# Where the score scale, the output bias, the zeros and the output tiles of a two-layer transformer are placed, with a new order table

## The chip, the cores and the metric

The kernel runs on one core of a Trainium2 chip. The metric is the device time of one execution in microseconds (us). Times of single parts come from one execution taken by the hardware profiler. Engines: TensorE (PE, and PEld for its weight loads), VectorE (DVE), ScalarE (ACT), GpSimd (POOL) and SyncE (SP, which here only issues transfers). L12 is line 12 of the kernel file of before.

## The reference

Two layers on x of 2 x 1024 x 256, everything in float32. The first is single-head causal attention with a residual, then a layer norm. The second is a block with 16 heads and a dense mixture of four experts, with residuals, then a layer norm again.

```python
x = layernorm(x + attn(x))            # one head, key size 256, gamma/beta on its input
h = x
z = layernorm(h) * ln1_w + ln1_b
q, k, v = z @ wq + bq, z @ wk + bk, z @ wv + bv     # 16 heads of 128
q, k = rope(q), rope(k)
p = softmax(causal(q @ k.T / sqrt(128)))
h = h + (p @ v) @ wo + bo
z = layernorm(h) * ln2_w + ln2_b
top2 = softmax of the two largest of softmax(z @ w_gate)
h = h + sum over 4 experts of top2[e] * (gelu(z @ we1[e] + be1[e]) @ we2[e] + be2[e])
out = layernorm(h)
```

## The kernel before

**Rows.** A row is one tile of 128 queries. The first layer has 16 (class RowA, 2 batches x 8), the second 256 (class RowB, 32 units of batch and head with 8 rows each, numbered 16 to 271). Two units of one group of weights and one batch make a pair of 16 rows. A row goes through `scores` (TensorE, L1206), a mask and the row's maximum (DVE, `softmax_row`, L678 and L680), `exponential` (ACT, L685), `normalise` (DVE's reciprocal L1221, ACT L1223), `transpose` (DVE, L721, 32x32 blocks into a place) and, for every four rows, `gather` (16 transfers issued by SP, L732, in two halves, which finish the transposition into pT) and `output` (TensorE, L1272; the result leaves PSUM through ACT with the value bias, L1288). The exponentials of three rows can be alive (`PR = 3` buffers named pr), the scores of two.

**Projections.** The second layer's wk, wq and wv are multiplied in 2x2 blocks with seven products instead of eight (`seven_products`, p1 to p7, L973 and L982, added up by DVE at L1015), and wo likewise (`seven_outputs`, L1130, added into h by DVE at L1139). The sums of weight blocks that they need are made on POOL (`weight_sums`, L949 to L952; `output_weight_sums`, L1099 to L1102), those of x by `x_sums`, those of the attention's output by `output_sums` (DVE). Only the first pair uses plain projections (`b_project`, `b_value`). After q or k is there, POOL rotates it for rope in pieces of 512 columns (`rotation`, four instructions, L897 to L899); the rows' scores read the rotated tiles Twq and Twk.

**What the change touches.** `scale_queries` multiplies the loaded block of wq by 1/sqrt(128) on POOL (L886); `parameters` copies the transposed parameter vectors from PSUM to the tile par (L588) and scales bq in it (L593). `h_load` brings one batch of the first layer's output from DRAM into h (SP, L856) and `h_bias` adds bo to one tile of h on POOL (L861, 16 times). The places into which the first layer's rows are transposed are set to zero by two memsets on POOL (L710). `a_norm` normalises x for the first layer (L560, DVE). `o_stats`, `m_rstd` and `o_finish` are the last layer norm of each tile: statistics on DVE (L551, L552), the reciprocal root on ACT (L556, L557), a factor on DVE (L1796), the application on ACT (L1801) and the output transfer issued by ACT (L1806). `expert` multiplies by we2 (L1769) and adds into h on DVE (L1778). `load_experts` (SP, L1567, 1 MB) and `load_second` (POOL's queue) bring the experts' weights.

**Order.** Engines run their instructions in the order in which they are issued. Every step above is appended to a list by `do` in a natural order (`at`, `late` and the like put it beside a row). Then a table moves single steps, each ahead of another one:

```python
def ordered(ops, moves):
    names = [key for key, _ in ops]
    for key, before in moves:
        names.remove(key)
        names.insert(names.index(before), key)
    by_name = dict(ops)
    return [by_name[key] for key in names]
```

Names read as in "RowB.gather 39 1" (row 39, second half), "wk.1.0 p4" (group 1, batch 0, product 4), "rotation 12" (the 13th piece rotated), "o_finish 1 1 3" (batch 1, second half, last tile).

Of the kernel before, what the change touches and what calls it, by code (L numbers as in the profile page):

```python
# [28 lines left out]
    ("o_finish 1 1 1", "o_stats 1 1 2"),  # L29
    ("m_rstd 1 4", "m_rstd 1 5"),  # L30
    ("all_of 1 1 1", "expert 1 1 2.0.3.0"),
    ("m_rstd 1 0.1.2.3 #2", "hidden 1 1 3"),
    ("o_stats 1 0 0.1.2.3", "hidden 1 1 1"),
    ("hidden 1 0 3", "m_bias 1 2.3"),
    ("o_stats 0 1 0.1.2.3", "m_bias 1 0.1"),
    ("hidden 1 0 2", "o_stats 0 1 0.1.2.3"),
    ("hidden 0 1 2", "all_of 0 1 1"),
    ("o_stats 0 0 0.1.2.3", "all_of 0 1 0"),
    ("m_rstd 1 4.5.6.7", "o_stats 0 0 0.1.2.3"),
    ("m_residual 1 0.1.2.3", "m_residual 0 0.1.2.3"),  # L40
    ("x1_back 1", "m_residual 1 0.1.2.3"),
    ("m_residual 0 4.5.6.7", "x1_back 1"),
    ("b_output 7 1 4.5", "hidden 0 1 1"),
    ("m_bias 0 6.7", "all_of 0 0 3"),
    ("RowB.output 271 99", "gate_products 1 2.3"),
    ("x1_back 0", "m_rstd 1 0.1.2.3"),
    ("RowB.transpose 271", "m_stats 1 0.1.2.3"),
    ("b_output 7 1 2.3", "RowB.normalise 271"),
    ("RowB.exponential 271", "RowB.output 263 9"),
    ("RowB.normalise 270", "RowB.transpose 269"),  # L50
    ("RowB.normalise 269", "RowB.transpose 268"),
    ("m_bias 0 0", "RowB.exponential 270"),
    ("RowB.output 263 8", "m_bias 0 0"),
    ("RowB.exponential 269", "hidden 0 0 1"),
    ("gate_weights 0", "load_weights 7 wo #2"),
    ("RowB.exponential 268", "gate_weights 0"),
    ("RowB.transpose 266", "gate_best 0 1"),
    ("RowB.normalise 267", "RowB.transpose 266"),
    ("RowB.output 259 8", "RowB.normalise 267"),
    ("RowB.gather 263 1", "RowB.normalise 266"),  # L60
    ("load_second 3", "RowB.gather 263 1"),
    ("RowB.transpose 265", "load_second 3"),
    ("b_output 6 1 6", "gate_products 0 6.7"),
    ("b_output 6 1 2", "RowB.gather 263 0"),
    ("gate_products 0 2.3", "b_output 6 1 0"),
    ("RowB.output 255 9", "gate_products 0 2.3"),
    ("RowB.transpose 263", "RowB.scores 265"),
    ("RowB.transpose 262", "m_transposed 0 1 1"),
    ("hidden 0 0 0", "RowB.transpose 262"),
    ("b_output 6 1 1", "RowB.output 255 8"),  # L70
    ("RowB.normalise 262", "b_output 6 1 1"),
    ("RowB.transpose 261", "RowB.scores 263"),
    ("gate_products 0 0.1", "RowB.normalise 261"),
    ("RowB.gather 259 1", "RowB.exponential 262"),
    ("RowB.transpose 260", "RowB.gather 259 1"),
    ("b_output 6 1 3", "RowB.scores 262"),
    ("RowB.transpose 259", "RowB.exponential 261"),
    ("m_transposed 0 0 0", "RowB.normalise 259"),
    ("m_transposed 0 0 1", "RowB.exponential 260"),
    ("wv.7.1 p5", "RowB.output 251 8"),  # L80
    ("RowB.gather 255 1", "m_norm 0 1"),
    ("m_stats 0 4.5.6.7", "RowB.normalise 257"),
    ("RowB.gather 255 0", "RowB.normalise 256"),
    ("wv.7.1 p4", "RowB.gather 255 0"),
    ("wv.7.1 p3", "wv.7.1 p4"),
    ("wv.7.1 p2", "RowB.output 247 10"),
    ("RowB.scores 257", "RowB.normalise 255"),
    ("RowB.exponential 256", "RowB.transpose 254"),
    ("m_norm 0 0", "RowB.exponential 256"),
    ("m_rstd 0 0.1.2.3", "m_norm 0 0"),  # L90
    ("RowB.scores 256", "m_stats 0 0.1.2.3"),
    ("RowB.output 247 8", "load_weights 6 wo #2"),
    ("RowB.transpose 252", "RowB.exponential 255"),
    ("RowB.gather 251 0", "RowB.gather 251 1"),
    ("RowB.exponential 254", "wo.7.0 12+c"),
    ("RowB.normalise 253", "RowB.transpose 251"),
    ("RowB.exponential 252", "RowB.normalise 253"),
    ("output_sums 7 0 3", "wo.7.0 12+a"),
    ("wo.7.0 22c", "wo.7.0 11b"),
    ("RowB.normalise 251", "wo.7.0 11a"),  # L100
    ("wq.7.1 p7", "rotation 125"),
    ("output_sums 7 0 2", "RowB.scores 251"),
    ("weight_sums wv #10", "output_sums 7 0 2"),
    ("RowB.scores 252", "RowB.gather 247 1"),
    ("wq.7.1 p6", "rotation 124"),
    ("RowB.scores 250", "RowB.gather 247 0"),
    ("RowB.exponential 249", "RowB.normalise 248"),
    ("RowB.transpose 247", "output_sums 7 0 0"),
    ("wq.7.1 p4", "RowB.transpose 247"),
    ("wq.7.1 p2", "load_weights 7 wv #2"),  # L110
    ("RowB.output 239 9", "wq.7.1 p2"),
    ("RowB.output 239 8", "rotation 122"),
    ("wq.7.1 p1", "RowB.output 239 8"),
    ("RowB.scores 248", "RowB.transpose 245"),
    ("rotation 121", "RowB.gather 243 1"),
    ("RowB.normalise 245", "RowB.transpose 244"),
    ("RowB.scores 247", "RowB.normalise 245"),
    ("RowB.scores 246", "RowB.normalise 244"),
    ("wv.0.1 p4", "wv.0.1 p3"),
    ("load_weights 2 wq", "rotation 29"),  # L120
    ("weight_sums wv #2", "load_weights 2 wq"),
    ("h_bias 1 4", "wv.1.1 p7"),
    ("RowB.output 39 10", "RowB.gather 47 0"),
    ("RowB.transpose 47", "wv.1.1 p3"),
    ("RowB.scores 50", "RowB.transpose 47"),
    ("RowB.transpose 46", "RowB.scores 50"),
    ("RowB.exponential 49", "wv.1.1 p4"),
    ("RowB.gather 43 1", "RowB.exponential 48"),
    ("wv.1.1 p2", "RowB.gather 43 1"),
    ("RowB.exponential 47", "wv.1.1 p1"),  # L130
    ("load_weights 1 wo", "RowB.scores 48"),
    ("RowB.output 39 9", "wo.0.0 21+a"),
    ("load_weights 0 wq", "RowB.output 39 9"),
    ("RowB.normalise 46", "load_weights 0 wq"),
    ("rotation 23", "RowB.normalise 46"),
    ("h_bias 1 6", "rotation 23"),
    ("RowB.exponential 46", "h_bias 1 6"),
    ("RowB.output 39 8", "wo.0.0 22+a"),
    ("h_bias 1 2", "RowB.output 39 8"),
    ("wo.0.0 12+c", "RowB.scores 46"),  # L140
    ("RowB.scores 47", "wo.0.0 12+c"),
    ("output_sums 0 0 3", "RowB.scores 47"),
    ("wo.0.0 12+a", "output_sums 0 0 3"),
    ("RowB.normalise 45", "RowB.normalise 44"),
    ("RowB.gather 43 0", "RowB.normalise 45"),
    ("h_bias 1 1", "RowB.scores 45"),
    ("RowB.normalise 43", "RowB.exponential 44"),
    ("RowB.exponential 43", "wo.0.0 11a"),
    ("h_bias 1 7", "wq.1.1 p7"),
    ("RowB.scores 44", "h_bias 1 7"),  # L150
    ("RowB.transpose 42", "RowB.scores 44"),
    ("h_bias 1 3", "RowB.transpose 42"),
    ("RowB.transpose 41", "h_bias 1 3"),
    ("h_bias 1 5", "RowB.transpose 41"),
    ("RowB.normalise 41", "h_bias 1 5"),
    ("RowB.normalise 42", "RowB.normalise 41"),
    ("RowB.exponential 42", "RowB.output 35 8"),
    ("rotation 21", "RowB.exponential 42"),
    ("h_bias 1 0", "rotation 20"),
    ("RowB.transpose 40", "h_bias 1 0"),  # L160
    ("output_sums 0 0 1", "RowB.gather 39 0"),
    ("wq.1.1 p2", "wq.1.1 p4"),
    ("RowB.exponential 41", "wq.1.1 p2"),
    ("RowB.normalise 39", "RowB.transpose 38"),
    ("RowB.normalise 40", "RowB.normalise 39"),
    ("RowB.output 31 10", "RowB.normalise 40"),
    ("output_sums 0 0 0", "RowB.output 31 10"),
    ("RowB.exponential 39", "wq.1.1 p1"),
    ("rotation 19", "RowB.exponential 39"),
    ("load_weights 0 wk", "rotation 19"),  # L170
    ("RowB.transpose 37", "load_weights 0 wk"),
    ("RowB.scores 40", "rotation 18"),
    ("RowB.scores 39", "RowB.scores 40"),
    ("RowB.output 31 8", "RowB.scores 39"),
    ("h_load 1", "wk.1.1 p7"),
    ("h_bias 0 7", "RowB.normalise 37"),
    ("rotation 17", "h_bias 0 7"),
    ("RowB.gather 35 1", "RowB.transpose 36"),
    ("h_bias 0 4", "RowB.transpose 35"),
    ("RowB.scores 38", "h_bias 0 4"),  # L180
    ("h_bias 0 5", "RowB.scores 38"),
    ("RowB.normalise 35", "h_bias 0 5"),
    ("RowB.normalise 36", "RowB.transpose 34"),
    ("wk.1.1 p5", "RowB.normalise 36"),
    ("wk.1.1 p6", "wk.1.1 p5"),
    ("h_bias 0 6", "wk.1.1 p6"),
    ("wk.1.1 p3", "h_bias 0 6"),
    ("wk.1.1 p4", "wk.1.1 p3"),
    ("h_bias 0 3", "wk.1.1 p1"),
    ("RowB.gather 31 1", "h_bias 0 3"),  # L190
# [183 lines left out]
def kernel(  # L374
# [334 lines left out]
    for z in blocks_a:  # L709
        nc.gpsimd.memset(z, 0.0)  # L710
# [1258 lines left out]
```

## Time and profile before

| | before |
|---|---|
| median of 4 runs | 1163.16 us (1157.45 to 1167.78) |
| the profiled execution, its own time | 1161.47 us |
| its span in the profile | 1159.6 us |
| mean granted TensorE clock | 0.994 |
| TensorE busy | 1131.6 us (98%) |
| DVE, ACT, POOL busy | 851.1, 645.1, 812.4 us (73%, 56%, 70%) |
| first layer | about 0 to 165 us |
| pairs of the second layer, each | 55.76 us, to about 1065 |
| last matmul to the end of the span | 7.0 us |

In the profile, "busy" counts the time in which an engine's instructions run. Slices are fortieths of the span with a digit for the busy share in tenths; PEclk is the clock granted to TensorE, in tenths of full speed. In a table by stretches each row names a stretch in us from the span's start, its length, the busy time and number of instructions of each engine, the granted clock, the share of the DMA engines and the GB/s that they moved. A line of waits reads: engine, operation and line that waited, what released it, and then the total us, how often, and the longest. A line of a timeline reads: start, duration, engine, line, operation, output and inputs.

### The profile page before, as it was taken

The numbers are of one execution on the slowest core, as the hardware profiler recorded it, in microseconds if no ns is written. First come the engines' busy times: TensorE is split into PE (matmuls) and PEld (weight loads), VectorE is DVE, ScalarE is ACT, GpSimd is POOL, SyncE is SP. The second block draws the span as 40 slices with busy tenths as digits, with TensorE's granted clock in tenths as the row PEclk, the third lists the DMA queues.
The fourth block names the chain that finished last, engine by engine and source line by source line (L and its number), as shares of the span: only waits on it lengthen the run. The fifth ranks groups of instructions, "written<-read, shape, count | busy, mean of one in ns | idle before, by whom it ended". The sixth has DMA issues, their size and how long they took to land.

```text
span 1159.6 us, 15853 instructions
## 1 busy us (share of the span) xinstructions
PE 1131.6 (98%) x4628; PEld 719.3 (62%) x4628; DVE 851.1 (73%) x1806; ACT 645.1 (56%) x1227; POOL 812.4 (70%) x762
## 2 busy tenths in 40 slices
PE   8999989999999999999999999999999999899997
PEld 5676645566666656565757575757565656566765
DVE  5657786868686868686878777787868687585575
ACT  3434566565656565656565666565665565462444
POOL 6006999999997989698969878888989997002100
PEclk9999999999999999999999999999999999899999
DMA  6142364756545554555455555555555748423011
GB/s 187 37 109 51 112 172 101 166 128 135 118 116 126 119 137 116 118 128 118 114 124 136 125 115 128 133 138 121 140 130 128 159 113 186 98 54 110 1 37 37
DMA packets 243223, 133.91 MB, mean 115 GB/s; under 512 B 18909, under 2 KB 241185, under 8 KB 242369
## 3 DMA queue, kind: packets, MB, share of 16 engines
q1 hardware_dynamic: 237952, 122.89, 45.6%
q0 software_dynamic: 1776, 4.89, 1.5%
q10 hardware_dynamic: 3408, 5.11, 1.2%
q8 instruction: 38, 0.62, 0.2%
q14 instruction: 49, 0.39, 0.1%
HBM read 22.71 MB, written 4.19 MB: 23 GB/s over the span
## 4 chain that ended last, share of the span: by engine, by line
PE 87%; POOL 5%; DVE 3%; DMA 1%; SPq 1%; ACT 1%; issue 1%; ACTq 0%; DVEq 0%; POOLq 0%
PE av L1272 20%; PE sc L1206 19%; PE pa L982 10%; PE pa L973 6%; PE pa L1130 5%; PE pa L1746 5%; PE pe L1769 4%; PE pc L982 4%; PE sc L751 3%; PE pc L973 2%; POOL rot L897 2%; PE pc L1130 2%; PE pa L800 1%; SPq L732 1%; PE pa L660 1%; PE pa L1082 1%
## 5 line engine op out<-in xcount | busy, mean ns | idle before, releaser
L1223 ACT ACTIVATE pr<-pr,rs 128x128 f32<-128x128 f32 (+5 forms) x252 | 195.7, 780 | 225.9 <-DVE rs L1221 225.9
L1206 PE MATMUL sc<-Twk,Twq 128*128 128x512 f32 (+3 forms) x768 | 289.4, 487 | 4.3 <-ACT pr L685 2.7
L1272 PE MATMUL av<-pT,vg 128*128 128x512 f32 (+3 forms) x768 | 270.8, 490 | 6.1 <-DMA pT<-pair_sb 6.1
L685 ACT ACTIVATE pr<-sc,nmx 128x256 f32<-128x256 f32 (+7 forms) x272 | 200.8, 738 | 120.3 <-DVE nmx L680 90.9
L1272 PEld LDWEIGHTS av<-pT,vg 128*128 128x128 f32 x768 | 143.6, 191 | 130.6 <-issue 95.8
L897 POOL TENSOR_TENSOR rot<-Twk,rope_sb 64x512 f32<-64x512 f32 x128 | 167.5, 1309 | 72.6 <-DVE Twk L1015 55.7
L1206 PEld LDWEIGHTS sc<-Twk,Twq 128*128 128x128 f32 x768 | 135.9, 191 | 124.6 <-issue 107.1
L680 DVE TENSOR_REDUCE nmx<-sc 128x1 f32<-128x128 f32 (+7 forms) x272 | 206.1, 758 | 9.4
L897 POOL TENSOR_TENSOR rot<-Twq,rope_sb 64x512 f32<-64x512 f32 x128 | 167.0, 1305 | 10.4 <-ACT Twq L925 1.7
L678 DVE TENSOR_TENSOR sc<-sc,limit 128x128 f32<-128x128 f32 x272 | 79.3, 292 | 97.4 <-PE sc L1206 77.3
L721 DVE STREAM_TRANSPOSE x<-pr 128x640 f32<-128x640 f32 (+1 forms) x124 | 128.5, 1036 | 21.5 <-ACT pr L1223 15.9
L898 POOL TENSOR_TENSOR Twk<-Twk,rope_sb 128x512 f32<-128x512 f32 x64 | 86.0, 1344 | 5.0
L899 POOL TENSOR_TENSOR Twk<-Twk,rot 128x512 f32<-128x512 f32 x64 | 85.6, 1337 | 5.0
L898 POOL TENSOR_TENSOR Twq<-Twq,rope_sb 128x512 f32<-128x512 f32 x64 | 82.1, 1283 | 5.0
L899 POOL TENSOR_TENSOR Twq<-Twq,rot 128x512 f32<-128x512 f32 x64 | 81.7, 1276 | 5.0
L1638 POOL TENSOR_TENSOR hx<-hx,x 128x256 f32<-128x256 f32 x16 | 11.5, 755 | 92.2 <-DMA x<-x_dram 74.6
L721 DVE STREAM_TRANSPOSE pair_sb<-pr 128x128 f32<-128x128 f32 (+1 forms) x120 | 59.9, 500 | 3.3 <-ACT pr L1223 1.9
L1139 DVE TENSOR_TENSOR hx<-hx,pa 128x512 f32<-128x512 f32 x70 | 46.6, 679 | 17.9 <-PE pa L1130 17.9
L1746 PE MATMUL pa<-xT,we_flat 128*128 128x512 f32 x128 | 58.2, 601 | 0.0
L1769 PE MATMUL pe<-lent,hT 128*128 128x256 f32 x240 | 54.4, 380 | 0.0
L1288 ACT ACTIVATE aT_sb<-av,par 128x512 f32<-128x512 f32 x64 | 43.7, 683 | 18.8 <-PE av L1272 14.6
L685 ACT ACTIVATION_READ_ACCUMULATOR pr<-sc,nmx 128x1 f32 x272 | 53.6, 197 | 0.0
(216 smaller groups left out, 1829.4 us busy)
## 6 DMA issues: line engine op xcount, KB each, us to landing
pT<-x SPq DMA_DIRECT2D x496, 128.0 KB, 2.7
pT<-pair_sb SPq DMA_DIRECT2D x480, 64.0 KB, 2.0
pT<-aT_sb SPq DMA_DIRECT2D x48, 128.0 KB, 3.1
pT<-za SPq DMA_DIRECT2D x48, 64.0 KB, 2.1
wq_g<-in_L_ffn_wq_dram SPq DMA_DIRECT2D x9, 256.0 KB, 3.1
wk_g<-in_L_ffn_wk_dram SPq DMA_DIRECT2D x9, 256.0 KB, 3.0
wv_g<-in_L_ffn_wv_dram SPq DMA_DIRECT2D x9, 256.0 KB, 3.0
wo_g<-in_L_ffn_wo_dram SPq DMA_DIRECT2D x9, 256.0 KB, 3.0
```

The costliest lines, as they stand in the source:

```text
L680: nc.vector.tensor_reduce(nmx, sc[:, :L], AX.X, ALU.max, negate=True)
L685: nc.scalar.activation(pr[:, :L], sc[:, :L], AF.Exp, bias=nmx, accum_out=sm)
L721: nc.vector.transpose(z[:, i % 4, :n, :], pr[:, : n * 32].rearrange("p (m s) -> p m s", s=32))
L897: nc.gpsimd.tensor_tensor(rot[lo, :], t[hi, cs], rope_sb[hi, 1, cs], ALU.mult)
L898: eng.tensor_tensor(t[:, cs], t[:, cs], rope_sb[:, 0, cs], ALU.mult)
L899: nc.gpsimd.tensor_tensor(t[:, cs], t[:, cs], rot, ALU.add)
L982: nc.tensor.matmul(pa, lhsT=w, rhs=x, start=start, stop=True, skip_group_check=True)
L1206: nc.tensor.matmul(sc[:, ds(n0, n)], lhsT=qT[:, ts(i, P)], rhs=kT[:, ds(n0, n)], start=True, stop=True,)
L1223: nc.scalar.activation(self.pr[:, :L], self.pr[:, :L], AF.Copy, scale=rs)
L1272: nc.tensor.matmul(cut(av), lhsT=vg[g, b][:, c, ts(hh, HD)], rhs=cut(pT[:, c, :]), start=(c == 0), stop=(c == i),)
L1746: nc.tensor.matmul(ph, lhsT=we1_sb[:, e, c, ts(m, P)], rhs=x2T[:, c, ds(k0 * P, 512)], start=(c == 0), stop=(c == DC - 1),)
L1769: nc.tensor.matmul(pe[:, ts(n, D)], lhsT=hTs[b, j, e][:, c, ts(k, P)], rhs=we2_sb[e][:, c, :], start=(c == 0), stop=(c == IC - 1),)
```

## The change

- **Scale.** `scale_queries` is gone. 128 to the power -1/4 (`ROOT_B`) is multiplied into ln1_w, ln1_b, bq and bk in the parameter tile, so the second layer's normalised input carries the factor and q and k each bear it once. v bears it too, and the attention's output takes it out again when it leaves PSUM.
- **bo.** `h_bias` is placed beside other rows: its 16 steps were moved by the old table to rows 26 to 48, and now stand beside rows 50–53, 66–69, 82–85 and 98–101, after the first addition into the tile.
- **Zeros.** Only the parts of the places that a gather reads and no transpose writes are set to zero, by six smaller memsets on DVE.
- **Output tiles.** Each half batch has its own output tile, whose parts are filled and sent. The very last tile is normalised by `ln_apply` on DVE and sent by SP.
- **Natural order.** a_norm 0 0 stands ahead of parameters 0. The experts 2 and 3 of the last tiles are separate steps, and m_rstd comes after o_finish of the tile before.
- **Order table.** MOVES is another list: the old one has 323 lines and the new one 261 in the diff, some of them shown.

```diff
@@ MOVES, from the end of the program to its start
-    ("o_finish 1 1 1", "o_stats 1 1 2"),
-    ("m_rstd 1 4", "m_rstd 1 5"),
-    ("all_of 1 1 1", "expert 1 1 2.0.3.0"),
+    ("o_finish 1 1 0", "expert 1 1 3.2"),
+    ("o_stats 1 1 1", "m_rstd 1 4"),
+    ("expert 1 1 3.1", "expert 1 1 3.0"),
...
-    ("RowB.gather 255 1", "m_norm 0 1"),
-    ("RowB.gather 255 0", "RowB.normalise 256"),
-    ("wv.7.1 p4", "RowB.gather 255 0"),
+    ("m_stats 0 0.1.2.3", "load_experts"),
...
+    ("RowB.exponential 174", "wq.5.0 p5"),
+    ("RowB.scores 174", "RowB.exponential 174"),
+    ("RowB.exponential 127", "wq.3.1 p5"),
+    ("RowB.scores 127", "RowB.exponential 127"),
+    ("RowB.exponential 91", "wq.2.1 p6"),
+    ("RowB.scores 91", "RowB.exponential 91"),
...
-    ("h_bias 1 6", "rotation 23"),
-    ("h_load 1", "wk.1.1 p7"),
-    ("RowB.gather 35 1", "RowB.transpose 36"),
+    ("RowB.gather 35 1", "output_sums 0 0 0"),
...
-    ("weight_sums wv", "rotation 10"),
-    ("output_weight_sums", "load_weights 1 wv"),
-    ("scale_queries #2", "a_residual 1 1"),
+    ("rotation 12", "RowB.normalise 26"),
+    ("a_apply 1 1 2.3", "RowB.scores 23"),
+    ("weight_sums wk", "a_residual 1 1"),
...
@@ scale
-    SCALE_B = 1.0 / math.sqrt(HD)
+    ROOT_B = HD**-0.25
@@ parameters
-            c = cols["bq"]
-            bq_par = par[:, c : c + wq.shape[1] // P]
-            nc.vector.tensor_scalar(bq_par, bq_par, SCALE_B, None, ALU.mult)
+            for lo, hi in (("ln1_w", "ln2_w"), ("bq", "bv")):
+                t = par[:, cols[lo] : cols[hi]]
+                nc.vector.tensor_scalar(t, t, ROOT_B, None, ALU.mult)
@@ zeros
-    for z in blocks_a:
-        nc.gpsimd.memset(z, 0.0)
+    for j, z in enumerate(blocks_a):
+        z = z.rearrange("p (c b x) -> p c b x", b=4, x=P)
+        for c in range(1, 4):
+            nc.vector.memset(z[:, 4 * j + c, :, : 32 * c], 0.0)
@@ scale_queries
-    def scale_queries():
-        t = wg["wq"].rearrange("p c n -> p (c n)")
-        nc.gpsimd.tensor_scalar(t, t, SCALE_B, None, ALU.mult)
@@ RowB.output
-            nc.scalar.activation(dst, src, AF.Identity, bias=par[:, bcol : bcol + 1])
+            nc.scalar.activation(
+                dst, src, AF.Identity, bias=par[:, bcol : bcol + 1], scale=1.0 / ROOT_B
+            )
@@ natural order of the start
+    do(a_norm, 0, 0)
     do(parameters, 0)
-    do(a_norm, 0, 0)
@@ h_bias
-            late(A0 + HL[b] + 3 + i, h_bias, b, i)
+            n = b * NT + i
+            late(A0 + HB + 2 * NT * (n // 4) + n % 4, h_bias, b, i)
@@ o_finish
-        o = xn_tile()
+        if (b, j) not in outs:
+            outs[b, j] = xn_tile()
+        o = outs[b, j][:, ks[0] : ks[0] + n, :]
...
+        last = (b, tiles[-1]) == (B - 1, NT - 1)
+        if last:
+            i = tiles[0]
+            ln_apply(
+                o[:, 0, :], h[:, b * NT + i, :], mv_h[b][:, i, 0:1], rstd_h[b][:, i : i + 1]
+            )
...
-        nc.scalar.dma_start(dst, o[:, :n, :])
+        (nc.sync if last else nc.scalar).dma_start(dst, o)
@@ natural order of the end
-        do(expert, 1, 1, [(2, k), (3, k)])
+        do(expert, 1, 1, [(2, k)])
+        do(expert, 1, 1, [(3, k)])
         do(o_stats, 1, 1, [k])
-        do(m_rstd, 1, [4 + k])
         if k:
             do(o_finish, 1, 1, [k - 1])
+        do(m_rstd, 1, [4 + k])
```

## The prediction

> **What bounds the kernel now.** I read the page's totals first, then its slices, the table by stretches, the waits of TensorE in the stretches where it sits idle, and the queues that it waits for there.
>
> ```profile
> span 1159.6 us, 15853 instructions
> PE 1131.6 (98%) x4628; PEld 719.3 (62%) x4628; DVE 851.1 (73%) x1806; ACT 645.1 (56%) x1227; POOL 812.4 (70%) x762
> POOL 6006999999997989698969878888989997002100
> PEclk9999999999999999999999999999999999899999
> PE 87%; POOL 5%; DVE 3%; DMA 1%; SPq 1%; ACT 1%; issue 1%; ACTq 0%; DVEq 0%; POOLq 0%
> ```
>
> TensorE is busy 98% of the span and carries 87% of the chain that ended last. POOL looks relaxed at 70%, but it is full from slice 4 on, and the chain runs through it for 5%. I priced each matmul by its usual distance to the next start in the trace (0.4295 us for 512 columns, 0.3225 for 384, 0.2155 for 256, 0.1115 for 128): 1115.7 us. The first starts at 3.5, 33.3 us lie lost between them, and 7.0 us follow the last: 1159.5. The changed order issues the same 4628 matmuls, so the 1115.7 stays. The question is which of the other 44 us go.
>
> ```profile
> core 0: us, PE busy (x) PEld busy (x) DVE busy (x) ACT busy (x) POOL busy (x), PEclk, DMA share, GB/s
> 120.00:140.00 20.00, 19.46 (x82) 14.65 (x80) 14.76 (x30) 10.89 (x23) 18.88 (x16) 1.00 0.32 103
> 140.00:180.00 40.00, 33.09 (x112) 17.47 (x113) 32.22 (x63) 25.55 (x48) 37.69 (x41) 1.00 0.62 153
> 220.00:250.00 30.00, 27.91 (x145) 20.14 (x144) 20.20 (x41) 15.82 (x30) 28.59 (x29) 0.94 0.62 132
> 350.00:930.00 580.00, 580.00 (x2455) 362.89 (x2454) 442.50 (x872) 349.29 (x668) 492.85 (x452) 1.00 0.55 128
> 980.00:1000.00 20.00, 16.02 (x50) 8.48 (x48) 8.77 (x19) 9.94 (x14) 0.44 (x1) 0.83 0.54 118
> ```
>
> Half of the program (350 to 930) loses nothing that shows here; by the distances it loses 0.24 us in each pair of units (55.76 us). The losses are 6.6 us before 20, 2.1 in 120–140, 7.3 in 140–180, 4.0 in 220–250, 1.5 in 930–960 and 6.9 in 980–1000. The waits of TensorE in three of these stretches:
>
> ```profile
> PE sc L1206 <- ACT pr L685: 2.0, 2, 1.4
> PE pc L982 <- POOL S L949: 1.9, 1, 1.9
> PE pt L566 <- DVE pair_sb L560: 1.8, 2, 1.0
> PE sc L1206 <- POOL Twq L899: 1.5, 1, 1.5
> ```
>
> **The opening, 105 to 177.** POOL has no gap here from rotation 2 (105.65) to the end of rotation 12 (177.05). Its queue holds six rotations, the scaling of wq, the sums of wk and wq, two rotations, the sums of wo and wv, three rotations:
>
> ```profile
> 139.30 1.49 POOL L886 TENSOR_SCALAR wq_g<-wq_g 128x512 f32<-128x512 f32 x1
> 140.88 0.46 POOL L949 TENSOR_TENSOR S<-wk_g 128x128 f32<-128x128 f32 x1
> 155.45 0.91 POOL L1099 TENSOR_TENSOR we_flat<-wo_g 128x128 f32<-128x128 f32 x1
> 175.79 1.26 POOL L899 TENSOR_TENSOR Twq<-Twq,rot 128x512 f32<-128x512 f32 x1
> ```
>
> The product p4 of wk waits for 140.88, behind the scaling, and the scores of row 32 for the last line. The change takes scale_queries out of this queue (1.57 with its gap) and puts the sums of wo and wv, 5.2 us (155.45 to 160.71), behind rotation 12; rotation 2 starts some 0.9 later, since TensorE reaches its projection 0.86 us of matmuls later. So rotation 12 ends near 177.05 + 0.9 − 1.6 − 5.2 = 171.1. The same matmuls that lie ahead of the scores of 32 take until 154.7 by distances alone. With POOL as the limit the offset is 171.1 − 154.7 ≈ 16.3, against 19.84 now: **−3.55** in all for 120–180. The waits for DVE's L560 and ACT's L685 shrink for nothing: POOL is late next. The output bias h_bias (16 x 0.73 = 11.3 us of POOL in 177–251) leaves this stretch too.
>
> What pays for it: h_bias comes back as four instructions (2.9 us) in each of the four pairs in about 270–430. POOL's fullest pair (263.00 to 318.76) is 52.56 busy of 55.76; less 1.49 for a scaling and plus 2.9 it is 54.0, so it fits, with 1.8 left. DVE's residual add (L1139) must wait for the h_bias of its tile, and DVE's softmax work stands behind it; the bias stands about 12 us ahead of the next add of the same batch, more than POOL's lag. Cover gone, it would cost up to 2.9 per pair. Value 0.
>
> **Scale.** The scaling runs 11 times, 16.4 us, but after 250 POOL is not waited for, so there it is worth nothing. In its place stand one DVE instruction on some columns of the parameters (L593's row is 0.17) and a scale operand in L1288's ACTIVATE (0.683, the same instruction): 0.
>
> **The start.** The zeros were two memsets on POOL, 1.82 and 3.53 us at 13.21 to 18.48; now six small ones stand on DVE, idle until 5.15. Not shown in the trace; between 6 x 0.17 and the whole 5.35 they end about when the first data come: 0 to +0.5, taken 0. a_norm 0 0 ahead of parameters 0 saves two DVE steps of 0.21, and a_norm 0 1 no longer runs 1630 ns beside the memset (405 usually): **−0.5**.
>
> **Gathers.** Two TensorE waits are for a gather of 16 transfers on SP, one at 226.4 and one at 984.9:
>
> ```profile
> PE av L1272 <- DMA pT<-pair_sb: 2.1, 1, 2.1
> PE av L1272 <- DMA pT<-pair_sb: 4.0, 1, 4.0
> ```
>
> The same stretches by clock (the figure before the DMA share) just after these waits:
>
> ```profile
> 230.00:233.50 3.50, 3.50 (x12) 2.39 (x11) 0.66 (x2) 0.29 (x2) 3.34 (x4) 0.51 0.11 25
> 988.00:994.50 6.50, 5.45 (x7) 2.35 (x8) 3.74 (x8) 3.43 (x5) 0.00 (x0) 0.50 0.39 93
> ```
>
> At 226.4 the attention output of rows 36–39 waits 2.25 us and the granted clock then falls to 0.5 for 3.4 us, 1.6 us more, plus 0.4 close by. Gather 35 starts at 199.9 and pushes gather 39 to 211.9–224.6. In the new order h_load 1 sits between the halves of gather 35, gather 35 starts near 192 and gather 39 has landed by 221, while TensorE comes to it after 223: **−4.1**. If only half of the lead is real the wait shrinks below 1: −3.
>
> *A rule against a row.* The Trainium skill, "TensorE: Matmul & The Clock Gate", section "HAM oscillation — how this bites in real kernels", has the clock fall back only after idle gaps of more than about 3.4 us. Here it fell after 2.25 us. By the rule closing the gap returns 2.25 and no clock, some 1.6 less; I keep the row.
>
> At 984.9 gather 255 (12.75 us of issue from 968.84, against 10.5 for others) shares the transfers with the 1 MB of expert weights issued just ahead of it; 4.15 idle and 2.7 of half clock follow. The new order leaves the load ahead of the gather, while TensorE arrives with 1.34 us less work before it and the gather some 0.4 earlier: **+0.9**. At 947 and 957 two short waits (0.69, 0.50) are broken up by other work put between: **−1.2**.
>
> **The tail.** The last matmul ends at 1152.66. The last tile's expert 3 is split off from expert 2, so one of two adds (0.5) moves under matmuls; the last tile goes through DVE, without L1796 (0.16), without the 0.47 that ACT's L1801 stood behind its predecessor and an issue, and its transfer goes out by SP, whose last gather is issued by about 1050. The landing stays (about 3 us): **−1.4**, between −1.0 and −1.9. Own places for output tiles free a wait that the trace does not show: 0.
>
> **The rest of the table.** From 350 to 930 rows and products are shuffled in some 15 pairs. At most 0.24 x 13 = 3 us can be won. Some rows (127, 174, 91) are scored up to four rows early and hold one of three pr buffers meanwhile; the row's chain through DVE and ACT takes 2.6 to 3.0 us, a row's period is 3.49, so it just fits. Bounds −3 and +4.3 (one stall like that at 226); taken **+2**, nearer the stall, since the row's margin is only half a microsecond.
>
> **Sum:** −3.55 − 0.5 − 4.1 + 0.9 − 1.2 − 1.4 + 2 = −7.9. The profiled execution took 1161.5 (span 1159.6 and 1.9 around it): 1153.6. The median of the four runs is 1163.2, 1.7 above; I put the median of the changed kernel about half of that higher, **1154.5**. Its own range is 1150 to 1159. One per cent is 11.6 us, about what a measurement of this kernel tells from no change: bounds 1151.5 and 1174.8.
>
> **Rivals.** *The wait at 985 goes too* (15%). For it: gather 255 needs only 4 us; against it: the load stays in front. −6.9 − 0.9 more: 1147. *POOL was not the limit of the opening* (15%): rows through DVE and ACT (32.22 of 40 busy) end last, −3.55 and −0.5 fall away: 1158.5. Against it: the chain names POOL's rotations from 160.7 to 177.1 without a break. *The filled pairs give it back* (16%): POOL at 54.0 of 55.76 lags in four pairs by 2 us each: 1162.5. *Slower* (12%): a row scored early takes the buffer, the row behind it exponentiates late, its gather starts late, and TensorE waits with a half-clock stretch after. One such stall costs 4.3 (2.25 + 1.6 + 0.4). From five of the 15 pairs on it decides: 5 x 4.3 = 21.5, 1176. Against it: DVE and ACT are 76% and 60% busy in 350–930, so a late row is caught up.
>
> **How the numbers follow.** The forecast has 42%. Below 1151.5 lie the first rival and a third of the forecast's own range: 30%. Above 1174.8 lies nearly all of the slow case: 12%. The rest, 58%, is within 1%. The range 1144 to 1168 leaves out the slow case and the lower end of the first rival.
>
> **What would show it.** Right: no L886 row; POOL's rotation 12 ends near 171 and TensorE's lost time before 180 falls from 16 to 12; no wait for a gather at 220–230 and one clock dip fewer; about 4 to 5 us idle still at 980–990; under 6 us after the last matmul. Wrong: TensorE waits on POOL in 270–430, or on gathers between 350 and 930, or no wait at 985.

## The result, and the profile after

The changed kernel takes 1161.39 us (median of 46 runs, 1158.54 to 1167.50) against 1163.17 (70 runs, 1157.20 to 1170.62): ratio 0.9981, interval 0.9968 to 0.9993. It is faster by 1.8 us, or 0.2%. Forecast were 8.7. The profiled execution took 1161.38, its span is 1159.5, 0.1 below that of before.

The page's totals, POOL's and the clock's slices and the chain that ended last, changed kernel:

```profile
span 1159.5 us, 15802 instructions
PE 1128.5 (97%) x4628; PEld 716.6 (62%) x4628; DVE 853.7 (74%) x1813; ACT 648.9 (56%) x1228; POOL 790.6 (68%) x749
POOL 4006999989897979697969778887989998002100
PEclk9999999999999999999999999999999999999999
PE 86%; DVE 8%; DMA 2%; issue 1%; POOL 1%; ACT 1%; SPq 1%; DVEq 0%; ACTq 0%; POOLq 0%
```

POOL fell from 5% of the chain to 1%, and DVE rose from 3% to 8%. What TensorE waits for is now mostly VectorE instead of POOL. The clock has no slice below 9 any more. The same stretches as before (start and length, then busy time and instructions by engine, granted clock, DMA share, GB/s):

```profile
20.00:120.00 100.00, 98.75 (x367) 64.77 (x366) 68.99 (x167) 38.46 (x91) 22.23 (x19) 1.00 0.28 66
140.00:180.00 40.00, 34.37 (x116) 18.00 (x115) 34.66 (x67) 28.80 (x56) 37.77 (x37) 1.00 0.60 151
220.00:250.00 30.00, 30.00 (x156) 21.03 (x155) 21.66 (x47) 17.41 (x34) 26.87 (x31) 1.00 0.68 137
350.00:930.00 580.00, 576.81 (x2435) 360.24 (x2434) 439.93 (x868) 349.09 (x665) 482.66 (x447) 1.00 0.55 126
980.00:1000.00 20.00, 16.44 (x64) 9.43 (x63) 11.03 (x24) 11.86 (x18) 2.29 (x3) 1.00 0.51 121
```

Before, the first of them read:

```profile
20.00:120.00 100.00, 100.00 (x379) 66.43 (x378) 69.60 (x172) 41.55 (x96) 27.75 (x23) 1.00 0.31 74
```

220–250 is full now, the dip at 980–1000 is smaller. But 20–120 and 350–930, which had been full, have holes: 1.25 and 3.2 us of TensorE. In the lost time of the prediction (matmul starts against their usual distances), us:

| stretch | before | after | difference | forecast |
|---|---|---|---|---|
| 0–20 | 6.6 | 6.1 | −0.5 | −0.5 |
| 20–120 | 0.4 | 3.2 | +2.8 | 0 |
| 120–180 | 9.4 | 7.4 | −2.0 | −3.55 |
| 180–250 | 4.7 | 1.1 | −3.7 | −4.1 |
| 250–920 | 3.8 | 8.8 | +5.0 | +2 |
| 920–960 | 1.5 | 2.9 | +1.5 | −1.2 |
| 960–1000 | 6.9 | 3.9 | −3.0 | +0.9 |
| last matmul to the end | 7.0 | 6.6 | −0.4 | −1.4 |

The profile of before holds three stretches of 3.41 us at half clock ahead of the last matmul (one at 230, two at 988), that of the changed kernel none. As the last section shows, such a stretch depends on where a wait falls in the execution, too.

TensorE's waits (what released it, total, times, longest), the main ones in 140–165, in 350–930 and in 900–1000:

```profile
PE sc L1143 <- ACT pr L624: 4.3, 4, 1.9
...
PE pa L919 <- DVE Twq L952: 3.2, 4, 1.5
...
PE av L1209 <- DMA pT<-pair_sb: 1.9, 1, 1.9
PE av L1209 <- issue: 1.9, 1, 1.9
PE pa L1685 <- DVE hx L1029: 1.7, 1, 1.7
```

Neither POOL's sums nor its rotations stand here any more. The scores wait for a buffer that an exponential frees, whose row waited for its mask on VectorE. The second line is product p7 of wq: TensorE waits for VectorE to empty a bank. The next two are the attention's outputs behind gathers 239 and 255; the second of them is put down to no engine. VectorE's queue ahead of such a wait, at 381 to 387 (start, duration, engine, line, operation, tiles):

```profile
382.81 1.75 DVE L1049 TENSOR_TENSOR aT_sb<-aT_sb 128x512 f32<-128x512 f32 x1
384.49 0.29 DVE L617 TENSOR_TENSOR sc<-sc,limit 128x128 f32<-128x128 f32 x1
384.81 0.69 DVE L619 TENSOR_REDUCE nmx<-sc 128x1 f32<-128x512 f32 x1
385.41 0.68 DVE L952 TENSOR_TENSOR Twq<-pc,part 128x512 f32<-128x512 f32 x1
```

The mask and the maximum of row 91, whose scores the new table puts ahead of p6, stand in front of the addition into Twq. In the trace of before that addition directly follows the 1.75 us one:

```profile
384.63 1.75 DVE L1112 TENSOR_TENSOR aT_sb<-aT_sb 128x512 f32<-128x512 f32 x1
386.31 0.68 DVE L1015 TENSOR_TENSOR Twq<-pc,part 128x512 f32<-128x512 f32 x1
```

### The profile page after: what moved, and what is told of

It reads as the page before. It is cut to its first block, busy times and chain, and to the rows that moved or that the text cites. A ratio compares the mean times of both kernels' runs of the same rounds, so it can differ in the third digit from the quotient of the medians.

```text
span 1159.5 us, 15802 instructions
## 1 busy us (share of the span) xinstructions
PE 1128.5 (97%) x4628; PEld 716.6 (62%) x4628; DVE 853.7 (74%) x1813; ACT 648.9 (56%) x1228; POOL 790.6 (68%) x749
## 4 chain that ended last, share of the span: by engine, by line
PE 86%; DVE 8%; DMA 2%; issue 1%; POOL 1%; ACT 1%; SPq 1%; DVEq 0%; ACTq 0%; POOLq 0%
PE sc L1143 19%; PE av L1209 18%; PE pa L919 10%; PE pa L910 5%; PE pa L1067 5%; PE pa L1685 5%; PE pe L1708 4%; PE pc L919 4%; PE pa L741 2%; PE sc L692 2%; PE pc L910 2%; PE pc L1067 2%; PE pa L599 1%; PE pa L586 1%; PE pa L1019 1%
## 5 line engine op out<-in xcount | busy, mean ns | idle before, releaser
L1160 ACT ACTIVATE pr<-pr,rs 128x128 f32<-128x128 f32 (+3 forms) x252 | 195.6, 778 | 187.8 <-DVE rs L1158 187.7
L624 ACT ACTIVATE pr<-sc,nmx 128x640 f32<-128x640 f32 (+7 forms) x272 | 201.2, 740 | 153.6 <-DVE nmx L619 120.0
L619 DVE TENSOR_REDUCE nmx<-sc 128x1 f32<-128x640 f32 (+7 forms) x272 | 206.1, 758 | 9.4
L1076 DVE TENSOR_TENSOR hx<-hx,pa 128x512 f32<-128x512 f32 x70 | 46.6, 679 | 13.8 <-PE pa L1067 13.7
L1225 ACT ACTIVATE aT_sb<-av,par 128x512 f32<-128x512 f32 x64 | 43.8, 685 | 20.5 <-PE av L1209 18.9
```

Source lines behind the costliest of these rows:

```text
L619: nc.vector.tensor_reduce(nmx, sc[:, :L], AX.X, ALU.max, negate=True)
L624: nc.scalar.activation(pr[:, :L], sc[:, :L], AF.Exp, bias=nmx, accum_out=sm)
L1160: nc.scalar.activation(self.pr[:, :L], self.pr[:, :L], AF.Copy, scale=rs)
```

## The experiments

Lost time of each run's profile, us. "Code, old order" and the like are the runs below; those for which no median is given were run once. Stretches that an edit doesn't reach agree mostly within 0.3, except where a half-clock stretch follows a wait in one run and not in another (about 1.6 us each). Two stretches scatter more: 250–920 loses 3.8 in before and 2.7 to 3.1 in four other runs with the old order and the early bias (only before waits 0.92 at 331), and 960–1000 loses 2.5 to 3.9 in the changed kernel and the runs with its order that have no half clock there.

| run | 0–20 | 20–120 | 120–180 | 180–250 | 250–920 | 920–960 | 960–1000 | span |
|---|---|---|---|---|---|---|---|---|
| before | 6.6 | 0.4 | 9.4 | 4.7 | 3.8 | 1.5 | 6.9 | 1159.6 |
| before + scale | 6.3 | 0.5 | 7.7 | 4.7 | 2.7 | 1.5 | 7.2 | 1156.6 |
| before + scale + late sums | 12.3 | 1.4 | 6.6 | 4.7 | 3.1 | 0.9 | 6.0 | 1161.1 |
| before + late bias | 6.4 | 0.4 | 9.5 | 3.1 | 4.5 | 1.5 | 4.1 | 1155.9 |
| before + zeros | 6.3 | 0.4 | 13.7 | 2.8 | 2.7 | 1.5 | 6.6 | 1159.8 |
| code, old order | 6.4 | 0.4 | 7.7 | 2.9 | 2.8 | 1.5 | 5.4 | 1152.1 |
| after | 6.1 | 3.2 | 7.4 | 1.1 | 8.8 | 2.9 | 3.9 | 1159.5 |
| after + scaling work | 6.1 | 3.2 | 8.2 | 1.6 | 8.2 | 2.7 | 3.1 | 1159.1 |
| after, early bias | 6.4 | 3.2 | 7.4 | 0.6 | 8.1 | 2.7 | 6.2 | 1160.7 |
| after, old opening | 6.2 | 0.4 | 8.3 | 1.3 | 8.6 | 4.0 | 3.6 | 1158.6 |
| after, x sums later | 6.8 | 3.2 | 6.0 | 0.0 | 7.8 | 4.1 | 3.9 | 1157.8 |
| after, natural middle | 6.1 | 3.2 | 7.4 | 1.0 | 4.4 | 1.5 | 4.7 | 1154.4 |
| after, gather 239 | 5.9 | 3.2 | 9.0 | 1.3 | 8.6 | 0.2 | 2.5 | 1156.5 |
| after, load split | 6.3 | 3.2 | 7.4 | 1.0 | 8.6 | 4.3 | 2.6 | 1159.3 |
| after, root first | 6.7 | 3.2 | 7.5 | 1.0 | 8.9 | 2.8 | 3.3 | 1158.7 |
| mixed order, split | 6.2 | 0.4 | 6.8 | 1.3 | 4.5 | 1.5 | −0.2 | 1145.4 |

**Is it the code or its order?** The changed code with the steps in the order of the kernel before:

```diff
 MOVES = (
-    (the new table)
+    (a table that gives the old order; the experts 2 and 3 of a tile stand next to each other)
 )
```

> The changed code in the old order: scale, zeros, output tiles and the DVE finish of the last tile as changed, all steps in the order of the kernel before (the bias early too, the experts 2 and 3 of a tile next to each other). Theory V (the table brought the new waits): lost time 350-930 is back at 2.2 us from 6.6, 20-120 at 0.4 from 3.2, while the waits at 226 (2.3 and the half clock) and 985 are as before; the tail after the last matmul is below 6 us, since the last reciprocal root stands ahead of the application of the tile before. Span about 1157, 2 to 3 below before. Rival (the moved work itself, not its order, makes the new waits): 350-930 stays at 5 or more.

Median 1153.87 of 7 runs, ratio 0.9903 (0.9868 to 0.9938): 6.5 us of lost time less than in the changed kernel and 0.9 less behind the last matmul. 350–930 is full again:

```profile
350.00:930.00 580.00, 580.00 (x2439) 361.33 (x2438) 442.12 (x871) 350.37 (x668) 482.08 (x443) 1.00 0.55 128
```

Theory V's points on 20–120, on 350–930 and on the tail came true. The waits at 226 and 985 stayed too, but 2.11 and 3.75 long and with less half clock behind them (none and 3.41 us), and the span was 5 lower than it said. The same code is worth 1%, and the new table gives most of it back.

**The middle of the table.** 79 of its lines, those beside rows 57 to 231, are taken out; three of them are shown.

```diff
-    ("wv.6.1 p3", "RowB.output 231 10"),
...
-    ("RowB.scores 91", "RowB.exponential 91"),
...
-    ("wq.0.1 p5", "output_sums 1 0 3"),
```

> The changed kernel without the 79 lines of the new table that move steps beside rows 57 to 231, which stand in their natural order again; the late bias stays. Theory V (rows whose scores were put ahead of products bring their mask and maximum into VectorE's queue ahead of the additions that free TensorE's banks): the waits of product p7 of wq at 273, 328, 385, 443, 778 and 836 (6.2 us together) fall to 0.15 each, but for 0.3 and 0.9 at the first two, as before; 250-930 loses 3.5 instead of 8. Theory H (the bias on POOL in rows 50 to 101 slows VectorE beside it): the four waits between 270 and 445 (4.5 us) stay, those at 778 and 836 go.

Median 1157.17 of 12 runs, ratio 0.9930 (0.9904 to 0.9956); 250–920 loses 4.4 instead of 8.8. The p7 waits at 328 and 385 fell from 1.56 and 1.63 to 0.43 each, that at 778 from 1.35 to below 0.2. Waits of TensorE in 250–400:

```profile
PE pa L840 <- DVE Twq L873: 1.1, 3, 0.6
```

So these lines cost 4.4 us; that the rows put forward among them do it is read from VectorE's queue above, not tested row by row. What is left over the old order's 2.7 to 3.1, with p7 waits of 0.74 and then 0.43 in the four pairs with the late bias instead of about 0.13, is the bias's share.

**The bias, both ways.** In the kernel before its sixteen steps were put where the changed kernel has them, and in the changed kernel back where they were.

```diff
+    ("h_bias 0 0", "RowB.scores 51"),     # before: late
...
+    ("h_bias 0 1", "RowB.transpose 26"),  # after: early
```

> The kernel before with nothing changed but the place of the sixteen bias additions: beside rows 50 to 101, as in the changed kernel. Two things are asked. Where the wait at 226 went (2.25 us and the half clock): if the bias on POOL made it, lost time 220-250 falls from 4.0 to below 1; if the order of h_load 1 and gather 35 made it, it stays at 4. And what the bias costs in its new place: by the prediction on record nothing (POOL has 1.8 us of slack in a pair); by theory H (POOL beside VectorE in the pairs) each p7 of wq in the four pairs after 270 waits 0.3 us or more longer, lost time 250-500 from 2.1 to above 3.3.

> The changed kernel with the sixteen bias additions back beside rows 26 to 48, all else as changed. Theory H: the p7 waits between 270 and 445 (0.86, 1.56, 1.63, 0.42) lose 0.3 each, 250-500 falls from 5.0 to about 3.8, and POOL, 11.3 us fuller in 177-250, makes rows wait there: 180-250 rises from 1.05 to 2 or more. Rival (the bias is hidden in both places): every stretch within 0.3 of the changed kernel.

In the kernel before, the late bias alone brings the wait at 226 down from 2.25 to 0.5 without half clock, for a new wait of 1.1 at 212.7: 180–250 falls from 4.7 to 3.1. In the changed kernel the early bias does not bring the wait back (0.6). So it takes both, the full POOL and the old order; the prediction named only the order (of gather 35 and h_load 1, which no run moves alone), and either change removes it. The late bias has a price where nothing was forecast: in the kernel before the p7 waits of the four pairs are 0.78, 0.41, 0.43 and 0.42, against 0.13 or so in the runs with the early bias. That makes 1.8 us in 250–920 against the 2.7 of two other runs of the old order, 0.7 against the profile of before with its wait at 331. In the changed kernel the early bias wins back 0.7. Whether POOL beside VectorE is the reason, as theory H says, is not shown.

**The scale, both ways.**

```diff
-        nc.gpsimd.tensor_scalar(t, t, SCALE_B, None, ALU.mult)   # before: gone
+        nc.gpsimd.tensor_scalar(t, t, 1.0, None, ALU.mult)       # after: back
```

> The kernel before with the scale moved and nothing else: the eleven POOL instructions of scale_queries are gone, the order of all other steps is the old one. Prediction on record: POOL is without a gap from 105 to 177, so its queue ends 1.57 us earlier and the lost time in 120-180 falls from 9.4 to about 7.9, the wait of p4 at 139.3 from 2.1 to 0.6. Theory V: p4's wait falls by 1.5, but TensorE meets VectorE's a_apply and the exponentials 1.5 us sooner at 146 to 151 and waits that much longer for them, so 120-180 falls by 0.5 or less. After 250 nothing in either.

> The changed kernel with the eleven POOL instructions of the old scaling put back (each multiplies wq by 1, 1.49 us; the second one stands ahead of the sums of wk as it did). Theory V (in the changed kernel VectorE's queue is what TensorE waits for in the opening, POOL stands about 0.7 us behind it): the lost time of TensorE in 120-180 rises from 7.4 us to between 8 and 8.5, since rotation 12 ends about 1.5 later (175.7) and only what exceeds the 0.7 shows; nothing changes after 250. Theory P (POOL is still the limit of the opening): the full 1.5, to 9. Theory 0 (the scaling was hidden in every place): below 0.3 more.

In the kernel before, p4's wait fell from 2.09 to 0.38 and 120–180 from 9.4 to 7.7: the 1.57 of the record, and theory V's half microsecond was wrong, since the later waits stayed as long as they had been. In the changed kernel the same work costs 0.75 there and 0.5 in 180–220, so part of it is hidden under VectorE. Another 1.1 us fewer after 250 is not put down to the scale, since the run with only the zeros moved shows the same.

**The sums of wo and wv behind rotation 12.** On top of the moved scale:

```diff
+    ("weight_sums wv", "h_bias 0 1"),
+    ("output_weight_sums", "wv.1.0 p1"),
```

> The kernel before with the scale moved (as in the run that did only that, where 120-180 lost 7.7 us instead of 9.4) and the POOL sums of wv and wo, 5.2 us, put behind rotation 12 as in the changed kernel. Prediction on record: POOL's queue reaches rotation 12 another 5.2 us earlier, so the wait of row 33's scores at 173.5 (1.7) goes and 120-180 falls to about 6. Theory V: VectorE, busy with the normalisation and the exponentials' masks, sets 140-160, and of POOL's 5.2 us only this last wait comes back: 5.4 in 140-160 stays as it is, 160-180 falls from 1.8 to below 0.5.

The wait of 1.7 for the last rotation went. The stretch fell by 1.1, where the record had 2. The waits of 140–160 did not shrink, as theory V says: there VectorE's normalisation and the exponentials come last. They stand 7 us later in this run, and 147–167 lost 6.0 where 140–160 had lost 5.4. (The 6 us more in 0–20 belong to the zeros, below.)

**VectorE in the opening.** Once the four sums of x for batch 1 were spread over rows 31 to 36; once the steps up to row 19 stood in the old order.

```diff
+    ("x_sums 1 2", "wk.1.1 p1"),
+    ("x_sums 1 1", "RowB.scores 36"),
...
+    ("x_sums 1 3", "RowB.scores 34"),
...
+    ("x_sums 1 0", "RowB.scores 32"),
```

> The changed kernel with the four sums of x of batch 1 (VectorE, 1.3 to 1.75 us each, three of them at 156 to 160.7 ahead of row 29's mask) spread over rows 31 to 36, ahead of the products that need them. Theory V: the waits at 156.0 and 160.7 (0.89 and 2.03) go, row 32 then waits for POOL instead, whose rotation 12 ended at 174.2, 0.7 before TensorE came; with VectorE no longer beside it POOL's rotations shrink by about 1 (3.27 back to 2.6 and alike), so that 140-180 falls by 1 to 1.7, from 7.45 to about 6.1. Theory P (POOL alone is the limit): no more than 0.7. If nothing behind limits: 2.9.

> The changed kernel with the steps up to row 19's scores in the order of the kernel before; the rest of the new table stays. Theory V: lost time 20-120 is back at 0.4 from 3.2, because the normalisation of the next tiles no longer stands ahead of the mask of row 15 and the copies of v in VectorE's queue; the three microseconds are kept after 120 in part only, since VectorE and POOL are full there: 120-180 rises from 7.45 to 8.5 or 9. Rival (they are all given back, as the limit of the whole opening is POOL's queue, which begins with rotation 2): 0-180 stays at 16.8.

The first brought 1.4 us in 120–180, inside the range of theory V; the wait of 2.03 at 160.7 went and a smaller one (0.85, for a gather) came at 170.6; and 180–250 lost nothing at all. The second brought 2.8 us in 20–120; 120–180 lost 0.9 more, but this run has a half-clock stretch at 150 that the changed kernel lacks, so that nothing need have been given back. The 3.2 us lost in 20–120 are thus the new table's work. In the changed kernel VectorE runs from 94.6 to 109.3 almost without a gap, with normalisations ahead of row 15's mask and of the copies of v that free TensorE's banks (two lines of VectorE's queue, then TensorE's waits in 98–108):

```profile
98.87 0.69 DVE L498 TENSOR_SCALAR pair_sb<-x,mva,rx 128x256 f32<-128x256 f32 x2
101.00 0.68 DVE L1013 COPY vg<-pa 128x512 f32<-128x512 f32 x1
PE pa L1006 <- DVE vg L1013: 0.5, 1, 0.5
PE pa L855 <- DVE vg L1013: 0.3, 1, 0.3
```

**Three single stalls.** Without the three lines that hold row 239 back; with the experts' load in two parts; with the last two roots ahead of the application of the tile before.

```diff
-    ("RowB.gather 239 1", "RowB.normalise 244"),
...
-    ("RowB.gather 239 0", "RowB.normalise 241"),
-    ("RowB.scores 242", "RowB.transpose 239"),
@@
+    def load_experts():
+        load_first(0, 1)                       # expert 0, ahead of gather 255
...
+    def load_rest():
+        load_first(1, E)                       # the other three, behind it
@@
+    ("m_rstd 1 7", "o_finish 1 1 2"),
+    ("m_rstd 1 6", "o_finish 1 1 1"),
```

> The changed kernel without three lines of the new table: the ones that put row 242's scores ahead of row 239's transposition and both halves of gather 239 behind rows 241 and 244. Theory: SP stood idle from 911.0 until row 239's transposition at 916.7, which row 242's mask and maximum had pushed back on VectorE; without them the gather starts about 2 us sooner, and the wait of the output of rows 236-239 at 930.8 (2.04 us) goes: 930-960 falls from 2.95 to about 1. Rival (SP's transfers are slow there because weights are loaded beside them, 11.99 us for 16 instead of 10.5): the wait stays above 1.3.

> The changed kernel with the experts' 1 MB loaded in two parts, expert 0 ahead of gather 255 and the other three behind it; nothing else moves. Theory: the waits at 986.8 and 990.6 (2.02 and 1.87 us; the second is for the bank that VectorE frees late, as its queue stands behind a transposition that waits for the same gather) go, 980-1000 falls from 3.9 to below 0.5. Rival (the gather is late because its second half is issued late, not because of the load): 3 or more stay.

> The changed kernel with the reciprocal roots of the last two tiles (m_rstd) ahead of the application of the tile before (o_finish) in ScalarE's queue; nothing else moves. Theory: the last root waits 1.28 us behind that application (mean and variance ready at 1154.52, the root began at 1155.69), so the time from the last matmul's end to the span's end falls from 6.6 to about 5.4. Prediction on record for the same stretch: 5.5 already in the changed kernel, so nothing would be left to win. Rival (the landing of the last transfer sets the end): within 0.2 of 6.6.

The wait at 930.8 was the table's: 920–960 fell from 2.9 to 0.2. With the split the wait for gather 255 was 0.64 instead of 2.02, but that does not show that the split did it: the gather's last part landed at 988.40, against 988.48 in the changed kernel, and TensorE came 1.3 us later. Without the split the same order shows waits of 0.46 to 2.26, and landings 15.3 to 17.1 us after the gather's start; with it 15.5. The wait at 990.6 (1.87) stayed, and its cause is open. The root came 1.22 us sooner and the end 0.8, since ScalarE's own last transfer, issued at 1155.53, now ends last. ScalarE's queue in the changed kernel:

```profile
1154.68 0.60 ACT L1748 ACTIVATE pair_sb<-hx,nb,rsh 128x256 f32<-128x256 f32 x1 [0.23 <-DVE nb L1744]
1155.31 0.34 ACTq L1753 DMA_DIRECT2D out_dram<-pair_sb  x1
1155.69 0.29 ACT L494 ACTIVATE rsh<-mvh,eps_t 128x1 f32<-128x1 f32 x1 [0.42 <-ACT pair_sb L1748]
```

The root of the last tile stands behind the tile before and its transfer, though its variance was ready at 1154.52.

**The zeros.** The kernel before with nothing moved but its zeros, from POOL to VectorE.

```diff
-        nc.gpsimd.memset(z, 0.0)
+        for c in range(1, 4):
+            nc.vector.memset(z[:, 4 * j + c, :, : 32 * c], 0.0)
```

> The kernel before with the zeros on VectorE as in the changed kernel, and nothing else. Theory L: the two POOL memsets begin 0.4 to 0.6 us after VectorE's first four a_norm instructions in the profiles of before, and where they begin sooner VectorE is held until they end (5.9 us in one profile of the old start). Then runs of before fall into two groups, and this kernel keeps only the lower one: all its runs below 1164, median near 1159, 4 to 8 below the median of before. Prediction on record: the zeros are worth nothing or half a microsecond, and the runs stay in both groups, median within 1 of before.

Median 1160.49 of 12 runs against 1167.24 of 17 beside it; ratio 0.9950 (0.9923 to 0.9976). All 12 lie at or below 1165.02 (one above the 1164 expected); of the 17, 11 lie at or above 1165.24. Of the 70 runs of before in the result, 38 lie below 1164 with a median of 1160.3 and 32 above it with a median of 1168.0. What parts the two groups shows in two profiles of the same old start, first of before and then of the run with scale and late sums (there is no profile of before itself in the upper group):

```profile
11.23 1.37 DVE L560 TENSOR_SCALAR pair_sb<-x,mvx,rsx 128x256 f32<-128x256 f32 x4
13.21 1.82 POOL L710 MEMSET za<- 128x2048 f32 x1
```

```profile
11.19 7.14 DVE L560 TENSOR_SCALAR pair_sb<-x,mvx,rsx 128x256 f32<-128x256 f32 x4
12.56 1.85 POOL L710 MEMSET za<- 128x2048 f32 x1
14.31 3.55 POOL L710 MEMSET aT_sb<- 128x4096 f32 x1
```

Where the memset begins 0.65 us sooner it meets the four normalisations, which then take 7.14 us in place of 1.37. It is the third of them that is held: it takes 6.16 us instead of 0.41 and ends at 18.01, 0.15 behind the second memset. The 1630 ns normalisation of before ends 0.16 behind it in the same way. The profile of before shown ahead of the prediction is one in which the memset came just too late to do so. The Trainium skill, "SBUF — State Buffer", section "SBUF: two separate sides", describes a pair of ports that VectorE and GpSimd hold in turn for a whole instruction. That the held normalisation ends just behind the second memset agrees with it; that it is recorded as starting 0.7 us ahead of the first memset, and stays held over two of them, the sentence alone does not explain.

**A mixed order.** The changed code, the old order to row 28 (with the sums of wo and wv behind rotation 12), the new one to row 57, the old one from there; the x sum in place later; the load split.

```diff
 MOVES = (
+    (old order to row 28, new to row 57, old to the end)
 )
+    ("x_sums 1 3", "RowB.scores 36"),
+    ("load_rest", the step behind "RowB.gather 255 1"),
```

> The changed code with an order made of both tables: the old order to row 28, but the sums of wo and wv behind rotation 12; the new order from there to row 57, with the late bias; the old order from row 57 to the end. The sum of x in place stands ahead of row 36, and the experts' 1 MB is loaded in two parts, expert 0 ahead of gather 255 and the other three behind it. Theory V, with the lost time of the parts as measured: 0-120 6.7, 120-180 6 to 7, 180-250 1, 250-930 4, 930-960 1.5, and at 985, where the gather shares its time with a quarter of the load, 2 instead of 6.9: 22 us in all, against 33.5 in the changed kernel and 27.0 in the changed code in the old order. With 5.6 behind the last matmul the span is 1147 and the time 1149. If the split of the load does nothing, 1153.

Median 1147.34 of 6 runs, ratio 0.9855 (0.9821 to 0.9889) to the kernel before. 20.5 us are lost in place of 33.5, and TensorE has no hole left at 985, where the six other profiles with the old order at the end wait 2.4 to 4.4 us. Gather 255's last part lands 13.9 us after the gather's start here, 17.2 to 19.2 there:

```profile
span 1145.4 us, 15866 instructions
980.00:1000.00 20.00, 20.00 (x89) 13.54 (x88) 12.88 (x40) 11.99 (x21) 0.00 (x0) 1.00 0.55 124
963.05 10.50 SPq L667 DMA_DIRECT2D pT<-x  x16
```

It beats both kernels, by 16 and 14 us.

## Why the prediction was right or wrong

**What bounds it** was read rightly: the matmul stream of 1115.7 us is the same in both, and only the time between matmuls moved.

**Start: right** (−0.5), but the zeros were mis-sized. They were priced at nothing, from one profile. As the run with the zeros alone shows, they are worth nothing in the runs of before's lower group and 6 to 8 us in the others (6.0 in the one profile, 7.6 between the groups); in the median that made 6 us there, where 11 of 17 runs lay in that group, and some 3 us in the result, where it was 32 of 70. This is also why the median fell by 1.8 while the two profiled spans are alike: before's was one of the lower group. Against that group alone (1160.3) the changed kernel is about 1 us slower. The row of 1630 ns beside the memset was the sign, and the margin between the first normalisations and the memset in that profile, 13.21 against 12.60, should have been read as a race.

**Opening: the term was mis-sized.** The scale gave its 1.57 (1.7 measured). The sums behind rotation 12 were to give 2 more and gave 1.1; in the changed kernel nothing of that is left, since VectorE is late next. The step that failed is the claim that the waits for L560 and L685 vanish because POOL's offset falls; the rival "POOL was not the limit" was half right. Rotation 2 began not 0.9 but 2.8 us later (108.47 for 105.65), behind the holes of 20–120, and rotation 12 ended at 174.2 instead of 171.1:

```profile
108.47 2.94 POOL L834 TENSOR_TENSOR rot<-Twk,rope_sb 64x512 f32<-64x512 f32 x2 [10.44 <-ACT Twk L862]
172.97 1.27 POOL L836 TENSOR_TENSOR Twq<-Twq,rot 128x512 f32<-128x512 f32 x1
```

TensorE reached row 32 only at 174.9, held up by the rows' masks and exponentials.

**20–120 was not in the sum at all.** Its work was taken as unchanged, but the table reorders it: +2.8, won back by the old order.

**Gathers: right in size, only partly in cause.** −3.7 against −4.1. In the kernel before the late bias alone is worth 1.6 of it.

**985: wrong sign.** −3.0 against +0.9. The gather began 2.7 us later and yet took 10.58 us to issue instead of 12.75; the load was 2.1 ahead of it instead of 1.4 (load and gather, first before, then after):

```profile
967.40 0.48 SPq L1567 DMA_DIRECT2D we_flat<-in_L_ffn_we_dram  x1
968.84 12.75 SPq L732 DMA_DIRECT2D pT<-x  x16
969.49 0.49 SPq L1504 DMA_DIRECT2D we_flat<-in_L_ffn_we_dram  x1
971.58 10.58 SPq L673 DMA_DIRECT2D pT<-x  x16
```

The waits themselves hardly changed, 4.15 in one before and 2.02 and 1.87 in two after; what went is the 2.7 of half clock. That the load beside the gather makes the wait is supported by the mixed order, which splits it and waits for nothing there; split in the changed kernel's order, it shows no clear gain.

**920–960: wrong.** The two short waits shrank to one of 0.45, and gather 239 came 2 us late: the late gather of the slow rival, once and in a place that I had not looked at, by steps put ahead of it and not by a held buffer.

**The rest of the table: right in sign, too small.** +5.0 in 250–920 against +2, outside the bounds (−3 to +4.3). Part of it is the late bias, which was given value 0 because POOL's pair still fits: it costs 0.7 to 1.8. The 79 lines of the table cost 4.4. For them I looked for rows that hold a buffer. What the queue shows is nearer: the row's mask and maximum, some 1 us, stand in VectorE's in-order queue ahead of the addition that frees a bank. Rows 127 and 174, which I named, left no wait at p7; without these lines the p7 waits beside rows 75 and 91 fell by 1.1 and 1.2, and the one at 778 by 1.2.

**Tail: wrong.** −0.4 against −1.4. I counted what the last tile no longer waits for and missed that the natural order puts its root behind the application of the tile before. That moved step costs 0.8 by the run with the root first; with the old order the tail fell by 1.3, about as forecast.

In one sentence: in the old order the code is worth 7.5 us of the span, more than the 3.5 that its parts had in the sum (two half-clock stretches that stayed away and the wait at 331 make up most of the difference), and the order table with the late bias, which had 4.4 of gain in the sum, costs 7.4 instead.

## What to carry to other kernels

When an order is rewritten, walk every in-order queue through every stretch that it touches, those that lose nothing now too: a step put ahead on one engine stands ahead of something else on another. Price a table of moves by running the old order on the new code; here that one run separated 1% of gain from its loss. And where two engines nearly collide in a profile, one execution shows only one of two outcomes: read the margin, and the spread of the runs.

## What the hardware showed that I had not expected

- A POOL memset that starts during VectorE's normalisations holds them until it ends: 7.14 us for four instead of 1.37, by a difference of 0.65 us in its start. Milder forms stand in the opening of the changed kernel: two normalisations took 1.68 us where four usually take 1.38, the second held until 0.15 us behind a POOL multiply of a rotation.
- TensorE's clock fell to about half for 3.4 us behind idle times far shorter than that, and not always. Waits of 2.15, 2.25, 2.26 and 2.38 us were followed by it; of those between 2.0 and 2.1 some were (2.10 at 139 in the run with the zeros) and some not (2.04 at 930.8 in the changed kernel), nor was one of 2.76 (at 931 in the run with the root first). Two waits of 1.65 and 0.61 close together were (early bias, at 149). The clock as the figure ahead of the DMA share, first for the 2.10, then for the 2.76, then for the two:

```profile
139.00:142.00 3.00, 1.06 (x3) 0.49 (x3) 2.97 (x8) 1.35 (x3) 2.75 (x4) 0.96 0.45 108
142.00:145.40 3.40, 3.40 (x5) 1.35 (x4) 1.01 (x2) 1.81 (x3) 3.17 (x7) 0.53 0.41 97
930.13:933.54 3.41, 1.55 (x4) 0.38 (x2) 0.78 (x2) 0.80 (x2) 2.95 (x3) 1.00 0.92 170
933.54:936.96 3.42, 2.68 (x7) 1.28 (x8) 2.38 (x5) 1.18 (x2) 3.26 (x3) 1.00 0.47 110
149.23:152.65 3.42, 1.48 (x8) 1.09 (x8) 3.39 (x9) 2.97 (x6) 3.26 (x3) 1.00 0.27 64
152.65:156.06 3.41, 3.41 (x6) 1.35 (x5) 3.34 (x8) 3.41 (x8) 3.19 (x4) 0.50 0.00 0
```

The clock records of the 16 profiles order this. In each, all changes of the granted clock lie on one grid of 3.413 us, and the grid's place differs from run to run. Add up TensorE's lost time in each step of the grid at full clock, up to the last matmul: all 21 steps with 2.15 us or more are followed by half clock, of those with 2.10 and 2.13 one is, and none with 2.06 or less. The wait of 2.76 is cut by the grid into 2.03 and 0.73; the waits of 1.65 and 0.61 lie in one step. So a stall near 2 us costs 2 or 3.6, by where it falls on the grid, and this alone moves equal kernels by some microseconds.
